# Sums in one PSUM bank in a seven-product down projection, and exponentials added by fours in every block of a transformer layer

## Chip, cores and metric

One Trainium2 chip; the kernel runs on one of its cores. The metric is device time in microseconds (us), the median of several runs. Engines: PE (TensorE, matmuls), DVE (VectorE), ACT (ScalarE), POOL (GpSimd), SP (SyncE, which issues most DMAs). A matmul writes PSUM, eight banks of 128 partitions x 512 float32; here four banks hold attention scores, one holds the attention accumulator, three ("lin") are shared by everything else.

## The reference

A pre-norm transformer layer in float32: x is (2, 1024, 1024), 32 heads of 32, FFN width 2752.

```python
def attn(x):
    qkv = (x @ qkvw + qkvb).reshape(B, S, 3, 32, 32)
    q, k, v = (qkv[:, :, i].transpose(0, 2, 1, 3) for i in range(3))
    probs = softmax(einsum('bhqd,bhkd->bhqk', q, k) / sqrt(32))
    ctx = einsum('bhqk,bhkd->bhqd', probs, v)
    return ctx.transpose(0, 2, 1, 3).reshape(B, S, H) @ ow + ob

def ffn(x):
    return (silu(x @ W_gate.T) * (x @ W_up.T)) @ W_down.T

x = x + attn(layernorm(x))
x = x + ffn(layernorm(x))
```

## The kernel before

The tokens are worked off in four blocks (batch b, half blk), 512 query tokens each. Attention of a block is 16 units of two heads; a unit has eight key tiles kt of 128 keys. For a key tile PE makes the scores (L510), ACT copies them to SBUF tile p (L529), DVE keeps the running maximum (L526). When all eight are there, DVE transposes and reduces the maximum (L549, L550), PE transposes it once more into a lin bank (L564), DVE reduces it to its negative (L565), and it goes through DRAM into a row m. Eleven key tiles behind the scores, `less_maximum` adds m (L580, on POOL, in the first block one of four on DVE), ACT takes the exponential (L589), and `values` multiplies with the values (L618).

The sum of the exponentials, the denominator of the softmax, comes from matmuls with a tile of ones into the other half of the same accumulator. To need fewer of these, neighbouring p tiles are first added in place (`add`, L603). In all blocks odd tiles take in the even one before them; in the first block (phase 0) every fourth tile also takes in the sum two tiles before it. The values are changed to match by `differences` (POOL, L594 and L597): if p1 holds p0+p1, then p0(v0-v1) + (p0+p1)v1 is what is wanted. So in phase 0 a run of four tiles needs four value calls and one call with ones, in phases 1 to 3 four and two (`summed`). Each call is four matmuls that run side by side in the array, of 256 columns. The adds are on DVE in phase 0; in phases 1 to 3 the add of kt 3 and 7 is on DVE, that of kt 1 and 5 on POOL.

The FFN of a block takes 21 chunks of 128 hidden rows and half a chunk, in parts of four chunks. A chunk is done by seven products of half size (Strassen in Winograd's form; L922, evicted mainly by DVE, L936 to L949), in place of eight. The down projection of the five whole parts is also done by seven products, each for two token tiles t (128 tokens), with two matmuls j of 512 columns each: `down7`, L1071. Its left factors are quarters of the hidden tile h and sums of them, which DVE makes in place in `sums_h` (L1040 to L1046). Each product goes into a lin bank of its own; DVE then adds it into the residual tile x in one or two places (`goes`: V1 to V4 are the four quarters of the output, product 1, 7 and 5 go to two of them; L1084, subtraction L1086). The part that is left over and the output projection are plain (L998, L780).

The order of the instructions of every engine is written out by the program: an `Emitter` interleaves a list of fill steps (projections, FFN) with the attention steps in equal beats. It runs a clock of estimated PE costs (`MM4` = 855 ns for one matmul of 512 columns), and `em.later(delay, ...)` emits a step once that clock has passed. The order of emission is the order of each engine's queue, which it works off in order. What has to wait for what, and which of a tag's buffers is free, is found by the tile framework from the uses of each tile. Attention of block 0 runs beside the projections, that of blocks 1 to 3 beside output projection and FFN of blocks 0 to 2; the FFN of block 3 is alone. Values of four tiles are emitted once the fourth is given as ("added", unit, kt), three beats after its `less_maximum`.

Weights of the down projection come by SP's queue into ten buffers of tag "D"; the list of loads follows `order`, and each matmul with t = 1 asks for the next load (`dst.next`).

Of the kernel before, what the change touches and what calls it, by code (L numbers as in the profile page):

```python
# [12 lines left out]
ALU = mybir.AluOpType  # L13
# [5 lines left out]
NH = 512  # L19
EPS = 1e-5  # L20
PART = 4
# [109 lines left out]
def preln_block_kernel(  # L131
# [14 lines left out]
    nc = tc.nc  # L146
# [13 lines left out]
    MM4, MM1 = 855.0, 230.0  # L160
# [36 lines left out]
    def lps(name, shape=(P, NH)):  # L197
        return psum.tile(list(shape), F32, tag="lin", bufs=3, name=name)
# [27 lines left out]
    WHOLE = (NFULL + 1) // PART  # L226
# [238 lines left out]
    class Unit:  # L465
# [111 lines left out]
        def less_maximum(self, kt):  # L577
            p = self.p[kt]
            eng = nc.vector if self.phase == 0 and kt % 4 == 3 else nc.gpsimd
            eng.tensor_tensor(p, p, self.m, ALU.add)  # L580
            em.later(3500.0, lambda: self.exponential(kt))
            if kt % 2 == 1:
                twice = self.phase == 0 and kt % 4 == 3
                em.later(8100.0, lambda: self.add(kt, 1), None if twice else ("added", self.n, kt))
                if twice:
                    em.later(9900.0, lambda: self.add(kt, 2), ("added", self.n, kt))
# [4 lines left out]
        def differences(self):  # L591

            v = self.v.rearrange("p (i a) n -> p i a n", a=2)
            nc.gpsimd.tensor_tensor(v[:, :, 0, :], v[:, :, 0, :], v[:, :, 1, :], ALU.subtract)  # L594
            if self.phase == 0:
                v = self.v.rearrange("p (i a) n -> p i a n", a=4)
                nc.gpsimd.tensor_tensor(v[:, :, 1, :], v[:, :, 1, :], v[:, :, 3, :], ALU.subtract)  # L597

        def add(self, kt, back):


            eng = nc.vector if self.phase == 0 or kt % RUN == RUN - 1 else nc.gpsimd
            eng.tensor_tensor(self.p[kt], self.p[kt], self.p[kt - back], ALU.add)  # L603

        def summed(self, kt):
            return kt % (4 if self.phase == 0 else 2) == (3 if self.phase == 0 else 1)

        def values(self, kt):


            if kt == 0:
                self.acc = psum.tile([P, NH], F32, tag="acc", bufs=1, name=f"acc_{self.name}")

            def columns(w, c, start, stop):
                for j in range(HPG):
                    part, h = divmod(j, 2)
                    q0 = h * NH + part * NQ
                    nc.tensor.matmul(  # L618
                        self.acc[j * HD : (j + 1) * HD, c : c + NQ],
                        w(h),  # L620
                        self.p[kt][:, q0 : q0 + NQ],
                        start=start,
                        stop=stop,
                        skip_group_check=True,
                    )

            v = lambda h: self.v[:, kt, h * HD : (h + 1) * HD]
            columns(v, 0, kt == 0, kt == NT - 1)
            if self.summed(kt):
                columns(lambda h: ones, NQ, False, kt == NT - 1)  # L630
            if kt == NT - 1:
                self.finish()
# [15 lines left out]
    def attention_steps(cuts):  # L648


        units = [Unit(n) for n in range(B * NS * UNITS)]
        lists = [Steps()]
        total = len(units) * NT
        q = lists[0]

        def load_step(k, i):
            if k < len(units):
                q.add(lambda: units[k].load(i), needs=("qk", units[k].b, units[k].g))

        for i in range(2):  # L660
            load_step(0, i)
        for n in range(total + NT + LAG + 3):
            if n in cuts:
                q = Steps()
                lists.append(q)
            k, kt = divmod(n, NT)
            if n < total:
                if kt == 1 or kt == 3:
                    load_step(k + 1, kt // 2)
                if n == 0:  # L670
                    q.add(lambda: em.later(9000.0, lambda: None, ("first",)))
                    q.add(lambda: None, needs=("first",))
                if kt == NT - 2:
                    q.add(units[k].load_v, needs=("v", units[k].b, units[k].hf))
            if n < total and kt % 2 == 0:
                q.add(lambda k=k, i=kt // 2: units[k].scores(i), MM4, beat=True)
            else:
                q.add(lambda: None, beat=True)
            k, kt = divmod(n - NT - LAG, NT)
            if 0 <= k < len(units):  # L680
                if kt == 0:
                    q.add(units[k].differences)
                q.add(lambda k=k, kt=kt: units[k].less_maximum(kt), needs=("max", k))
            k, kt = divmod(n - NT - LAG - 3, NT)
            if 0 <= k < len(units) and kt % RUN == RUN - 1:
                q.add(lambda: None, needs=("added", k, kt))
                for v in range(kt - RUN + 1, kt + 1):
                    cost = MM4 / 2 * (1 + units[k].summed(v))
                    q.add(lambda k=k, v=v: units[k].values(v), cost)
        return lists  # L690

# [155 lines left out]
    def ffn_steps(q, b, blk, st, turn):  # L847
# [36 lines left out]

        plain = {1: (0, 0), 2: (1, 0), 3: (1, 1)}
        dsums = {5: 0, 6: 1, 7: 2, 4: 3}
        order = (1, 2, 4, 7, 5, 6, 3)
        for pi in range(len(parts)):
            if pi < WHOLE:
                for n in order:  # L890
# [133 lines left out]
        def release(t, i):  # L1024
            x0, x1, x2, x3 = halves(t)
            if i == 0:
                nc.vector.tensor_tensor(x2, x3, x2, ALU.subtract)
            else:
                nc.vector.tensor_tensor(x1, x1, x3, ALU.add)
# [5 lines left out]
        def sums_h(pi, i):  # L1035
            a11, a12 = quarter_of(pi, 0, 0), quarter_of(pi, 0, 1)
            a21, a22 = quarter_of(pi, 1, 0), quarter_of(pi, 1, 1)
            if i == 0:
                st["s3"] = Sm(f"s3_{b}_{blk}_{pi}").rearrange("p (c n) -> p c n", c=2)
                nc.vector.tensor_tensor(st["s3"], a11, a21, ALU.subtract)  # L1040
            elif i == 1:
                nc.vector.tensor_tensor(a21, a21, a22, ALU.add)
            elif i == 2:
                nc.vector.tensor_tensor(a11, a21, a11, ALU.subtract)
            else:
                nc.vector.tensor_tensor(a12, a12, a11, ALU.subtract)  # L1046
# [7 lines left out]
            6: lambda pi: quarter_of(pi, 0, 0),  # L1054
            3: lambda pi: quarter_of(pi, 0, 1),
        }
        V1, V2, V3, V4 = (0, 0), (0, 1), (2, 0), (2, 1)
        goes = {
            1: ((V1, ALU.add), (V4, ALU.add)),
            2: ((V1, ALU.add),),  # L1060
            4: ((V3, ALU.add),),
            7: ((V2, ALU.subtract), (V4, ALU.add)),
            5: ((V3, ALU.add), (V4, ALU.add)),
            6: ((V4, ALU.add),),
            3: ((V2, ALU.add),),
        }

        def down7(pi, n, t, j):
            if j == 0:
                st["pd"] = lps(f"pd{n}_{b}_{blk}_{pi}_{t}")  # L1070
            nc.tensor.matmul(  # L1071
                st["pd"],
                lefts[n](pi)[:, j, t * P : (t + 1) * P],
                st["wp", pi, n, j],
                start=(j == 0),
                stop=(j == PART // 2 - 1),
            )
            if t == 1:
                dst.next()
            if j == PART // 2 - 1:  # L1080
                for (u, hf), op in goes[n]:
                    xs = st["x", t + u][:, hf * NH : (hf + 1) * NH]
                    if op == ALU.add:
                        nc.vector.tensor_tensor(xs, st["pd"], xs, op)  # L1084
                    else:
                        nc.vector.tensor_tensor(xs, xs, st["pd"], op)  # L1086

        def down_steps(pi):
            if pi < WHOLE:
                for n in order:  # L1090
                    for t in range(2):
                        for j in range(PART // 2):
                            q.add(lambda n=n, t=t, j=j: down7(pi, n, t, j), MM4)
                        if n == 3 and pi == WHOLE - 1:
                            q.add(lambda t=t: release(t, 0))
                    if n in (1, 2, 4, 7):
                        q.add(lambda i=(1, 2, 4, 7).index(n): sums_h(pi, i))
                return


            for hf in range(NHF):
                for t in range(TB):
                    for ci in range(len(parts[pi])):
                        q.add(lambda hf=hf, t=t, ci=ci: down(pi, hf, t, ci), MM4)
                    if hf == 0 and t < 2:
                        q.add(lambda t=t: release(t, 1))
# [246 lines left out]
```

## Time and profile before

| | us |
|---|---|
| median of 3 runs (lowest to highest) | 3282.67 (3280.46 to 3286.37) |
| the profiled execution | 3281.96 |
| its span, first to last instruction | 3280.2 |
| PE busy | 3217.5 (98%) |
| DVE busy | 1920.4 (59%) |
| POOL busy | 1758.6 (54%) |
| ACT busy | 1431.2 (44%) |
| mean granted TensorE clock | 0.994 |

The profile is of one execution. A group of instructions is told by its line in the kernel, its engine and its tiles (out<-in). "Busy" is the time in which at least one instruction of the group or engine ran. Matmul ends are modelled, with a tail that overlaps the next matmul, so distances between starts tell the rate better than durations. A float32 matmul shows as two records. A wait is the idle time of an engine just before an instruction, with the line that ended it.

### The profile page before, as it was taken

The numbers are of one execution on the slowest core, as the hardware profiler recorded it, in microseconds if no ns is written. First come the engines' busy times: TensorE is split into PE (matmuls) and PEld (weight loads), VectorE is DVE, ScalarE is ACT, GpSimd is POOL, SyncE is SP. The second block draws the span as 40 slices with busy tenths as digits, with TensorE's granted clock in tenths as the row PEclk, the third lists the DMA queues.
The fourth block names the chain that finished last, engine by engine and source line by source line (L and its number), as shares of the span: only waits on it lengthen the run. The fifth ranks groups of instructions, "written<-read, shape, count | busy, mean of one in ns | idle before, by whom it ended". The sixth has DMA issues, their size and how long they took to land. (4 is left out here: it accounts for less than half of the span.)

```text
span 3280.2 us, 43732 instructions
## 1 busy us (share of the span) xinstructions
PE 3217.5 (98%) x16320; PEld 1801.1 (55%) x16320; DVE 1920.4 (59%) x2478; ACT 1431.2 (44%) x1570; POOL 1758.6 (54%) x871
## 2 busy tenths in 40 slices
PE   8999999999999999999999999989999999999999
PEld 4444444444347655663466556634655566477775
DVE  2265676666356766666666666676666664344334
ACT  2244554444455545563655455545555554010000
POOL 0267776876676655568665555667765665200000
PEclk9999999999999999999999999999999999999999
DMA  4556766655534445446344444463444444544442
GB/s 155 171 184 193 226 192 203 200 180 161 158 99 135 142 151 146 146 146 200 107 142 145 139 141 137 145 192 110 137 145 146 146 138 140 184 151 153 153 152 97
DMA packets 337826, 507.29 MB, mean 155 GB/s; under 512 B 105424, under 2 KB 122064, under 8 KB 337616
## 3 DMA queue, kind: packets, MB, share of 16 engines
q1 hardware_dynamic: 281424, 405.91, 40.3%
q10 hardware_dynamic: 56192, 98.60, 9.8%
q8 instruction: 130, 2.13, 0.3%
q14 instruction: 80, 0.66, 0.1%
HBM read 429.14 MB, written 75.24 MB: 154 GB/s over the span
## 5 line engine op out<-in xcount | busy, mean ns | idle before, releaser
L580 POOL TENSOR_TENSOR p<-p,m 128x1024 f32<-128x1024 f32 x480 | 1180.8, 2483 | 13.6 <-DMA m<-d 13.4
L529 ACT COPY p<-s 128x1024 f32<-128x1024 f32 x512 | 516.7, 1011 | 872.1 <-DVE top L526 664.5
L526 DVE TENSOR_TENSOR top<-s,top 128x1024 f32<-128x1024 f32 x384 | 468.1, 1219 | 289.0 <-PE s L510 280.0
L589 ACT ACTIVATE p<-p 128x1024 f32<-128x1024 f32 x512 | 532.2, 1057 | 234.7 <-POOL p L580 206.8
L922 PE MATMUL p<-sum,m 128*128 128x256 f32 x2688 | 617.8, 383 | 4.9 <-DVE sum L904 3.3
L603 POOL TENSOR_TENSOR p<-p,p 128x1024 f32<-128x1024 f32 x96 | 227.2, 2367 | 658.9 <-ACT p L589 598.3
L922 PEld LDWEIGHTS p<-sum,m 128*128 128x128 f32 x2688 | 503.2, 190 | 124.7 <-issue 43.0
L922 PE MATMUL p<-xn2T,m 128*128 128x256 f32 x2016 | 473.5, 384 | 1.9 <-ACT gate L934 1.3
L370 PE MATMUL pq<-xnT,wqk 128*128 128x512 f32 x1024 | 463.7, 601 | 0.0
L1071 PE MATMUL pd<-wp,h 128*128 128x512 f32 x960 | 442.3, 607 | 8.3 <-DVE x L1084 6.4
L922 PEld LDWEIGHTS p<-xn2T,m 128*128 128x128 f32 x2016 | 378.2, 191 | 98.5 <-issue 45.4
L603 DVE TENSOR_TENSOR p<-p,p 128x1024 f32<-128x1024 f32 x192 | 306.2, 1595 | 134.1 <-ACT p L589 134.0
L370 PEld LDWEIGHTS pq<-xnT,wqk 128*128 128x128 f32 x1024 | 187.2, 190 | 252.8 <-issue 249.0
L1071 PEld LDWEIGHTS pd<-wp,h 128*128 128x128 f32 x960 | 179.3, 193 | 242.5 <-issue 203.4
L510 PE MATMUL s<-q,k 32*128 32x512 f32 x2048 | 300.8, 645 | 7.1 <-ACT p L529 7.0
L1084 DVE TENSOR_TENSOR x<-pd,x 128x512 f32<-128x512 f32 x360 | 236.9, 681 | 86.8 <-PE pd L1071 86.7
L618 PE MATMUL acc<-p,vals 128*32 128x256 f32 x4096 | 266.0, 383 | 1.8 <-DVE p L603 1.8
L1184 POOL TENSOR_TENSOR ws<-raw 128x512 f32<-128x512 f32 x62 | 93.7, 1512 | 299.9 <-DMA raw<-in_w_gu 170.5
L432 PE MATMUL pvv<-wv,xnT 128*128 128x512 f32 x512 | 233.3, 600 | 1.5 <-ACT xnT L266 1.5
L780 PE MATMUL po<-wo,ctx 128*128 128x512 f32 x512 | 234.6, 607 | 0.0
L618 PEld LDWEIGHTS acc<-p,vals 128*32 128x32 f32 x4096 | 120.1, 110 | 143.6 <-issue 70.2
L950 ACT ACTIVATE gate<-gate 128x512 f32<-128x512 f32 x84 | 52.9, 630 | 278.4 <-DVE gate L949 278.0
(96 smaller groups left out, 2451.3 us busy)
## 6 DMA issues: line engine op xcount, KB each, us to landing
m<-dws SPq DMA_DIRECT2D x336, 256.0 KB
m<-in_w_gu SPq DMA_DIRECT2D x252, 256.0 KB
wp<-ddn SPq DMA_DIRECT2D x160, 256.0 KB
m<-d SPq DMA_DIRECT2D x64, 512.0 KB
wp<-in_w_dn SPq DMA_DIRECT2D x120, 256.0 KB
raw<-in_w_gu ACTq DMA_DIRECT2D x84, 256.0 KB
dws<-ws ACTq DMA_DIRECT2D x84, 256.0 KB
x<-in_x SPq DMA_DIRECT2D x32, 512.0 KB
```

Of the source, the lines that this page charges most:

```text
L370: nc.tensor.matmul(ps, wqk[b, g, w, hk][:, k, :], xnT[b, s][:, kc, :], start=(kc == 0), stop=(kc == KC - 1),)
L510: nc.tensor.matmul(ps[a][:, h * NH : (h + 1) * NH], self.k[rows, i * P : (i + 1) * P], self.q[rows, :], start=True, stop=True,)
L526: nc.vector.tensor_tensor(self.top, s, self.p[0] if kt == 1 else self.top, ALU.max)
L529: nc.scalar.copy(self.p[kt], s)
L580: eng.tensor_tensor(p, p, self.m, ALU.add)
L589: nc.scalar.activation(self.p[kt], self.p[kt], AF.Exp, scale=SCALE)
L603: eng.tensor_tensor(self.p[kt], self.p[kt], self.p[kt - back], ALU.add)
L618: nc.tensor.matmul(self.acc[j * HD : (j + 1) * HD, c : c + NQ], w(h), self.p[kt][:, q0 : q0 + NQ], start=start, stop=stop, skip_group_chec ...
L780: nc.tensor.matmul(st["ps"], ctxT[b, blk][:, g, t * P : (t + 1) * P], st["w"][hf, g], start=(g == 0), stop=(g == G - 1),)
L922: nc.tensor.matmul(ps, mats[c, n][:, kc, :], rhs, start=(kc == 0), stop=(kc == hk - 1),)
L1071: nc.tensor.matmul(st["pd"], lefts[n](pi)[:, j, t * P : (t + 1) * P], st["wp", pi, n, j], start=(j == 0), stop=(j == PART // 2 - 1),)
L1084: nc.vector.tensor_tensor(xs, st["pd"], xs, op)
```

## The change

In attention, `add` by fours is done in all phases, so `differences` has its second subtraction and `values` has one call with ones for four tiles everywhere. Which engine does which add stays: the new second add (of kt 3 and 7, phases 1 to 3) is on DVE, emitted 9.9 us after `less_maximum`, and gives "added", which the first gave at 8.1 us.

In the down projection each output now gets one eviction for a bank, and three products add into the bank of another: 2 on top of 1, 6 on top of 7, 4 on top of 5. A bank is read after its first product (product 1 into V4, 7 from V2, 5 into V4), then the second product is accumulated on it (start=False), and it is read once more (1+2 into V1, 7+6 into V4, 5+4 into V3). The order of products is a list of turns (product, t), so that two other products stand between the two of a bank; (7, 0) and (2, 0) are one step, between which nothing else is emitted. The four sums of `sums_h` are emitted before the first product and behind (1, 0), (1, 1) and (2, 1), instead of behind products 1, 2, 4 and 7. The weights are loaded in the new order.

```diff
             if kt % 2 == 1:
-                twice = self.phase == 0 and kt % 4 == 3
+                twice = kt % 4 == 3
                 em.later(8100.0, lambda: self.add(kt, 1), None if twice else ("added", self.n, kt))
                 if twice:
                     em.later(9900.0, lambda: self.add(kt, 2), ("added", self.n, kt))
...
-            if self.phase == 0:
-                v = self.v.rearrange("p (i a) n -> p i a n", a=4)
-                nc.gpsimd.tensor_tensor(v[:, :, 1, :], v[:, :, 1, :], v[:, :, 3, :], ALU.subtract)
+            v = self.v.rearrange("p (i a) n -> p i a n", a=4)
+            nc.gpsimd.tensor_tensor(v[:, :, 1, :], v[:, :, 1, :], v[:, :, 3, :], ALU.subtract)
...
-            if self.summed(kt):
+            if kt % 4 == 3:
                 columns(lambda h: ones, NQ, False, kt == NT - 1)
...
-        order = (1, 2, 4, 7, 5, 6, 3)
+        order = (1, 2, 7, 6, 5, 4, 3)
...
         goes = {
-            1: ((V1, ALU.add), (V4, ALU.add)),
-            2: ((V1, ALU.add),),
-            4: ((V3, ALU.add),),
-            7: ((V2, ALU.subtract), (V4, ALU.add)),
-            5: ((V3, ALU.add), (V4, ALU.add)),
-            6: ((V4, ALU.add),),
-            3: ((V2, ALU.add),),
+            1: (V4, ALU.add),
+            2: (V1, ALU.add),
+            7: (V2, ALU.subtract),
+            6: (V4, ALU.add),
+            5: (V4, ALU.add),
+            4: (V3, ALU.add),
+            3: (V2, ALU.add),
         }
+        on_top = {2: 1, 6: 7, 4: 5}
+
+        turns = (
+            [(1, 0)], [(1, 1)], [(7, 0), (2, 0)], [(2, 1)], [(7, 1)], [(6, 0)], [(5, 0)], [(6, 1)],
+            [(5, 1)], [(4, 0)], [(3, 0)], [(4, 1)], [(3, 1)],
+        )
 
         def down7(pi, n, t, j):
-            if j == 0:
-                st["pd"] = lps(f"pd{n}_{b}_{blk}_{pi}_{t}")
+            key = "pd", on_top.get(n, n), t
+            if j == 0 and n not in on_top:
+                st[key] = lps(f"pd{n}_{b}_{blk}_{pi}_{t}")
             nc.tensor.matmul(
-                st["pd"],
+                st[key],
                 lefts[n](pi)[:, j, t * P : (t + 1) * P],
                 st["wp", pi, n, j],
-                start=(j == 0),
+                start=(j == 0 and n not in on_top),
                 stop=(j == PART // 2 - 1),
+                skip_group_check=True,
             )
...
-                for n in order:
-                    for t in range(2):
+                q.add(lambda: sums_h(pi, 0))
+                sums_behind = {(1, 0): 1, (1, 1): 2, (2, 1): 3}
+
+                def go(pair):
+                    for n, t in pair:
+                        for j in range(PART // 2):
+                            down7(pi, n, t, j)
+
+                for pair in turns:
+                    if len(pair) > 1:
+                        q.add(lambda pair=pair: go(pair), PART * MM4)
+                    else:
+                        n, t = pair[0]
                         for j in range(PART // 2):
                             q.add(lambda n=n, t=t, j=j: down7(pi, n, t, j), MM4)
-                        if n == 3 and pi == WHOLE - 1:
-                            q.add(lambda t=t: release(t, 0))
-                    if n in (1, 2, 4, 7):
-                        q.add(lambda i=(1, 2, 4, 7).index(n): sums_h(pi, i))
+                    if pair[-1] in sums_behind:
+                        q.add(lambda i=sums_behind[pair[-1]]: sums_h(pi, i))
+                    if pair[-1][0] == 3 and pi == WHOLE - 1:
+                        q.add(lambda t=pair[-1][1]: release(t, 0))
                 return
```

More of the change, by code (lines that the diff above doesn't have):

```diff
@@ L603, in add @@
             eng.tensor_tensor(self.p[kt], self.p[kt], self.p[kt - back], ALU.add)
-        def summed(self, kt):
-            return kt % (4 if self.phase == 0 else 2) == (3 if self.phase == 0 else 1)
         def values(self, kt):
@@ L687, in attention_steps @@
                 for v in range(kt - RUN + 1, kt + 1):
-                    cost = MM4 / 2 * (1 + units[k].summed(v))
+                    cost = MM4 / 2 * (1 + (v % 4 == 3))
                     q.add(lambda k=k, v=v: units[k].values(v), cost)
@@ L1080, in down7 @@
             if j == PART // 2 - 1:
[L1081 to L1086, printed above, removed]
+                (u, hf), op = goes[n]
+                xs = st["x", t + u][:, hf * NH : (hf + 1) * NH]
+                if op == ALU.add:
+                    nc.vector.tensor_tensor(xs, st[key], xs, op)
+                else:
+                    nc.vector.tensor_tensor(xs, xs, st[key], op)
         def down_steps(pi):
             if pi < WHOLE:
-                for n in order:
-                    for t in range(2):
+                q.add(lambda: sums_h(pi, 0))
[7 more added lines that the diff above has]
+                        q.add(lambda pair=pair: go(pair), PART * MM4)
+                    else:
+                        n, t = pair[0]
                         for j in range(PART // 2):
                             q.add(lambda n=n, t=t, j=j: down7(pi, n, t, j), MM4)
-                        if n == 3 and pi == WHOLE - 1:
-                            q.add(lambda t=t: release(t, 0))
-                    if n in (1, 2, 4, 7):
-                        q.add(lambda i=(1, 2, 4, 7).index(n): sums_h(pi, i))
+                    if pair[-1] in sums_behind:
+                        q.add(lambda i=sums_behind[pair[-1]]: sums_h(pi, i))
+                    if pair[-1][0] == 3 and pi == WHOLE - 1:
+                        q.add(lambda t=pair[-1][1]: release(t, 0))
                 return
```

## The prediction

> **What bounds the kernel now.** I read four views in this order: busy time by stage, the groups of instructions by shape, TensorE's own waits, and the order of time around single blocks. By stage (columns: length, then busy us and instruction count of PE, weight loads, DVE, ACT, POOL, then granted clock, DMA share, GB/s):
>
> ```profile
> 160.00:790.00 630.00, 625.75 (x2894) 259.86 (x2893) 407.28 (x378) 302.82 (x331) 456.94 (x242) 1.00 0.63 196
> 790.00:2800.00 2010.00, 1965.57 (x11290) 1149.08 (x11289) 1273.55 (x1664) 1059.45 (x1134) 1262.38 (x593) 0.99 0.48 143
> 2795.00:3280.00 485.00, 481.35 (x1736) 325.70 (x1728) 198.05 (x364) 29.27 (x56) 22.95 (x19) 1.00 0.46 147
> ```
>
> The first row is attention of the first block beside the projections, the second is attention of the other three blocks (48 units) beside output projection and FFN of the first three, the third is the last FFN alone. PE is busy 97.8% of the long stage and 99% of the others; DVE is at 63%, POOL at 63% there. So PE's work sets the time: a matmul taken away is a gain, DVE or POOL work matters only where PE comes to wait for it. How much PE waits in the long stage, and for whom:
>
> ```profile
> PE top L564 <- DVE part L550: 15.5, 9, 3.0
> PE pd L1071 <- DVE x L1084: 7.1, 12, 1.4
> PE s L510 <- ACT p L529: 7.0, 5, 2.6
> ...
> PE acc L618 <- DVE p L603: 1.5, 1, 1.5
> ```
>
> All of it is 44 us, and it is DVE being late for single moments, not DVE being full. A second price hangs on it: after some of these stalls the clock is halved. This stretch behind a stall shows it:
>
> ```profile
> 1821.33:1824.70 3.37, 2.86 (x4) 1.31 (x5) 3.24 (x6) 0.00 (x0) 0.00 (x0) 0.50 0.02 7
> ```
>
> The stall was 2.03 us and 3.4 us at half clock followed, so some 1.7 us of matmul time was lost behind it. Between 790 and 2800 us there are nine such stretches, six of 3.4 and three of 6.8 us, some 20 us in all; three of the short ones (1821, 1948, 2033 us; 5 us lost) lie in down projections. The Trainium skill's "TensorE: Matmul & The Clock Gate", section "Why this matters for your kernels", asks for no gap above about 3 us, since one idle window drops the clock; here stalls of 1.62, 2.03 and 2.70 us were followed by half clock, so by the page the downs would lose no clock at all, by the rows 5 us, and the rows decide.
>
> **The ones matmuls.** A run of four value tiles with its sums looks so, first in the last blocks (pairs, two calls with ones), then in the first (fours, one call):
>
> ```profile
> 2431.57 1.07 PE L618 MATMUL acc<-p,vals 128*32 128x256 f32 x16
> 2432.46 0.61 PE L618 MATMUL acc<-p,ones 128*32 128x256 f32 x8
> 2432.89 1.05 PE L618 MATMUL acc<-p,vals 128*32 128x256 f32 x16
> 2433.76 0.61 PE L618 MATMUL acc<-p,ones 128*32 128x256 f32 x8
> 2434.30 1.13 PE L922 MATMUL p<-xn2T,m 128*128 128x256 f32 x4
> ```
>
> ```profile
> 415.83 1.94 PE L618 MATMUL acc<-p,vals 128*32 128x256 f32 x32
> 417.58 0.61 PE L618 MATMUL acc<-p,ones 128*32 128x256 f32 x8
> 418.13 2.84 PE L370 MATMUL pq<-xnT,wqk 128*128 128x512 f32 x6
> ```
>
> From start to the next group: 2434.30-2431.57 = 2.73 us against 418.13-415.83 = 2.30 us, and 2.728 and 2.296 are the medians of the 96 and 32 such runs. The first becomes the second, 48 units x 2 runs = 96 times: 96 x 0.432 = **41.5 us less PE**. The other end is the busy time of the group below: 768 of 1792 records of 137.7 us are 59 us, but that counts the overlapped tail of every call, so I take 41.5.
>
> **What the fours cost.** Durations from the groups by shape:
>
> ```profile
> L603 DVE TENSOR_TENSOR p<-p,p 128x1024 f32<-128x1024 f32 x192 | 306.2, 1595 | 134.1 <-ACT p L589 134.0
> ...
> L1084 DVE TENSOR_TENSOR x<-pd,x 128x512 f32<-128x512 f32 x360 | 236.9, 681 | 86.8 <-PE pd L1071 86.7
> ...
> L618 PE MATMUL acc<-p,ones 128*32 128x256 f32 x1792 | 137.7, 379 | 0.0
> ...
> L597 POOL TENSOR_TENSOR vals<-vals 128x128 f32<-128x128 f32 x16 | 12.5, 782 | 1.3
> ```
>
> 96 more DVE adds at 1.60 us are 153 us of DVE. Beside POOL they vary (median 1.22, longest 3.44). The Trainium skill's "SBUF — State Buffer", section "Who interferes with whom", speaks against the edit: a DVE instruction with two SBUF inputs and a GpSimd one that reads SBUF block each other wholly. As an estimate by that page, with POOL 63% busy in instructions of 2.4 us, an add would wait 0.63 x 1.2 = 0.75 us on 1.22, 1.97 us each, 189 us in all; the row's mean is 1.60, so 153, and the row decides.
>
> Where does the second add (9.9 us after the subtraction, where the first stands at 8.1) touch PE? First at the value matmuls that read it: in the trace their distance from the end of the add has a median of 5.1 us over 96 runs, and four are under 2 us (0.05, 1.18, 1.78, 1.95). Moved back by some 1.9 us these would wait 1.9+0.7+0.1 = 2.7 us: **+3 us**. Then behind it on DVE's queue stand the evictions of the FFN products (0.42 us each). A product lasts 1.73 us and its PSUM buffer is wanted two products later; the time between eviction and reuse was under 1.3 us in 7 of 108 cases in each of the three blocks, at least 0.1, else mostly above 2.2 us. About 21 of 32 second adds of a block fall among products; each holds up one or two evictions: 21 x 1.5 x 7/108 = 2 hits of half a us, three blocks: **+3 us**. If all 96 adds hit, it would be 96 x 0.5 = 48 us, the end I keep for a rival. The negated maximum (L565) also stands behind the add; its row m has POOL waiting 5.0 us in the long stage and is wanted some five beats later, so nothing. POOL's 48 more differences are 48 x 0.78 = 38 us, covered by the 598 us that POOL waits for ACT's exponentials; without that cover up to 38 us of POOL, not of PE.
>
> **The down projection.** 28 matmuls a part before and after, so no PE work changes. DVE loses three evictions for each t: 20 parts x 2 x 3 = 120 x 0.68 = 82 us, 61 us of them in the long stage. There DVE goes from 1273 to 1273+153-61 = 1365 of some 1972 us, 69%: fuller, not the bound. The new waits: the second product of a bank starts after DVE has read the first. A quiet row of the last block, where DVE has nothing else, shows how long that takes:
>
> ```profile
> 3021.48 0.69 DVE L1084 TENSOR_TENSOR x<-pd,x 128x512 f32<-128x512 f32 x1 [0.94 <-PE pd L1071]
> ```
>
> The product that it evicts ends at 3021.28, so the bank is free 0.89 us later. With two products between there are 3.43 us, as with three buffers before. The one shorter place: with banks A and B held for products 1, and C by (7,0), (7,1) needs A after the eviction of (2,0), with only (2,1), 1.72 us, between; slack 0.83 us. In the last block that is enough. In the 15 parts beside attention a maximum (1.22 us) may stand ahead: 0.4 us on average, **+6**; four of them have the transpose of the maximum after three or four products, where it now waits for A, about 1 us each: **+4**. Against it, the double evictions of products 7 and 5 go, behind which evictions ended 3 to 5 us after their product; the stalls of later products in these rows (0.1 to 1.6 us, some 7 us, with one half-clock stretch 1.7) go, and some 1 us each where the transpose waited 2.03 and 2.70: **-10**. So the downs come to 0; ends -20 (all 15 us of stalls and 5 of clock gone, nothing new) and +56 (below). The pair glued together lets attention's steps wait up to 3.4 us; scores come every 10 us and their PSUM is freed about 6 us after, so a hit is rare: **+1**. The first h sum moves ahead of product 1: 0.7 us DVE, under 3.4 us of slack. The reordered weight loads keep their number and 10 buffers; PE waited 1.4 us once for one, so nothing.
>
> **Sum.** 3281.96 (span 3280.2 and 1.8 around it; the median of the runs is 3282.67) - 41.5 + 3 + 3 + 0 + 1 = **3247 us**, -1.1%; its own range 3230 to 3268.
>
> **Rivals.** (1) *The bank wait takes over*, 13%: in each of the 15 parts beside attention, between (2,0) and (7,1) or at the transpose, DVE is some 2 us late and half clock follows: 15 x (2.0+1.7) = 56 us, 3303 us. It decides from (41.5-7)/15 = 2.3 us for a part. For it: 2.03 and 2.70 us stalls in such parts, and three banks with two held. Against: S steps that brought maxima before these evictions now come behind the glued pair, and the sums before them are not more than now. (2) *DVE's fuller queue*, 9%: the 96 adds each cost PE 0.35 us among products: +34, 3281 us, no change. For: 69% busy in order. Against: margins above 2.2 us in most cases. (3) *The relief counts*, 12%: all stalls in the downs go: 3247-20 = 3227 us. For: backlogs of 4 to 5 us behind products 7 and 5. Against: the early ones come from maxima. That the saved evictions alone bring nothing is part of the forecast, for they were hidden.
>
> **How the numbers follow.** Forecast 66%, rivals 13, 9 and 12. The time is the forecast's, 3247. The range goes from 3226 (rival 3's middle; about 6% below) to 3284 (rival 1 and a little of rival 2 above, 14%). Beyond 0.2%, about what a measurement of this kernel can tell from none (3276 to 3289): faster 66+12+2 = 80%, within 7%, slower 13%.
>
> **What would show it.** Ones records 1024 instead of 1792 and every run of values at 2.30 us; L603 on DVE 288 times; evictions of pd 280 instead of 400, and PE's busy time down by about 41. Right if PE's waits stay near 45 us in the long stage; rival 1 shows as pd waiting on x after (2,0) with more half-clock stretches, rival 2 as p L922 waiting for gate or up evictions. A loss of PE time outside waits and clock would make all this wrong.

## The result, and the profile after

The changed kernel takes 3315.38 us (median of 4, 3314.23 to 3321.16), the kernel before 3281.57 us beside it (median of 4): a ratio of 1.0105, 95% interval 1.009 to 1.012. It is about 34 us slower; the forecast was 35 us faster, and the stated range ended at 3284.

| us | before | after |
|---|---|---|
| profiled execution | 3281.96 | 3314.23 |
| its span | 3280.2 | 3312.4 |
| PE busy | 3217.5 | 3199.3 |
| DVE busy | 1920.4 | 2002.3 |
| POOL busy | 1758.6 | 1799.7 |
| mean granted TensorE clock | 0.994 | 0.987 |
| PE waits beside attention of blocks 1 to 3 | 44 | 95 |
| lost in half-clock stretches there (half of their length) | 20 in 9 | 44 in 18 |

The last three rows hold the result. The stages after, in the same columns as before (length; busy us and count of PE, weight loads, DVE, ACT, POOL; clock, DMA share, GB/s):

```profile
160.00:790.00 630.00, 626.31 (x2895) 259.44 (x2894) 409.99 (x380) 304.08 (x333) 456.36 (x243) 1.00 0.62 197
790.00:2830.00 2040.00, 1944.73 (x10519) 1126.12 (x10518) 1370.68 (x1672) 1058.56 (x1132) 1304.00 (x640) 0.98 0.46 141
2845.00:3310.00 465.00, 463.62 (x1689) 317.62 (x1687) 169.97 (x316) 27.41 (x54) 17.99 (x15) 1.00 0.45 146
```

The first and last stage are as they were. The long one is where the time went, and DVE is not full in it: 1371 of 2040 us, 67%. Three groups, by shape:

```profile
L602 DVE TENSOR_TENSOR p<-p,p 128x1024 f32<-128x1024 f32 x288 | 473.0, 1642 | 136.4 <-ACT p L589 136.0
...
L1090 DVE TENSOR_TENSOR x<-pd,x 128x512 f32<-128x512 f32 x240 | 164.2, 685 | 127.7 <-PE pd L1076 127.3
...
L614 PE MATMUL acc<-p,ones 128*32 128x256 f32 x1024 | 80.1, 385 | 0.0
```

Ones records fell from 1792 to 1024, the adds rose by 96, the evictions at this line fell by 120: the change does what it says. PE's busy time fell by 18 us and not by the 41 given as a sign: matmuls at half clock take longer, and 24 us more were lost so. All 128 runs of values now last 2.30 us in the median. PE's waits in the long stage, after (us in total, times, longest):

```profile
PE acc L614 <- DVE p L602: 33.0, 18, 8.9
PE pd L1076 <- DVE s L1036: 29.0, 10, 4.2
PE top L564 <- DVE part L550: 9.7, 4, 3.5
...
PE pd L1076 <- DVE x L1090: 1.0, 2, 0.8
```

Two waits are new: the fourth value tile waits for the second add (before: 1.5 us), and product 7 waits for the first h sum s3 (before: nothing). Waits for evictions, which rival 1 was about, are 1.0 us, less than the 7.1 before. The books of the two profiled executions close: 41.5 us of ones matmuls went, 95-44 = 51 us of waits and 44-20 = 24 us of clock came, together +33; the span grew by 32.2.

**Product 7.** The order of time at the start of one down projection, first PE, then DVE, then POOL:

```profile
1722.15 3.60 PE L1076 MATMUL pd<-wp,h 128*128 128x512 f32 x8
1728.71 3.78 PE L1076 MATMUL pd<-wp,s 128*128 128x512 f32 x4 [2.97 <-DVE s L1036]
...
1722.35 0.42 DVE L945 TENSOR_TENSOR gate<-p,gate 128x256 f32<-128x256 f32 x1 [0.77 <-PE p L918]
1724.32 1.58 DVE L948 TENSOR_TENSOR h<-gate,up 128x512 f32<-128x512 f32 x1 [1.55 <-ACT gate L946]
1725.83 2.83 DVE L1036 TENSOR_TENSOR s<-h 128x512 f32<-128x512 f32 x1
...
1720.70 10.17 POOL L580 TENSOR_TENSOR p<-p,m 128x1024 f32<-128x1024 f32 x4
```

PE has two products (1, 0) and (1, 1), 3.43 us, and then wants s3. But s3 stands on DVE behind the end of the chunk just finished: DVE waits for ACT's silu, multiplies (L948), and only then comes to s3, whose inputs were ready a chunk before. On top both instructions are stretched, to 1.58 and 2.83 us, beside four POOL instructions in a row. In the last block, where POOL has little to do, the same order is quiet, and s3 is there 0.8 us before PE wants it:

```profile
2975.63 0.69 DVE L948 TENSOR_TENSOR h<-gate,up 128x512 f32<-128x512 f32 x1 [0.70 <-ACT gate L946]
2976.24 0.68 DVE L1036 TENSOR_TENSOR s<-h 128x512 f32<-128x512 f32 x1
...
2977.74 1.88 PE L1076 MATMUL pd<-wp,s 128*128 128x512 f32 x4
```

The 15 first sums of the long stage had a mean of 2.03 us, against 0.73 at their old place, and fall into two kinds. Ten overlapped POOL and took 1.51 to 2.85 us: these are the ten for which PE waited. The other five did not overlap POOL and took 0.68 to 0.69 us, and PE did not wait for them. Behind the stall shown first the clock was halved:

```profile
1728.10:1734.70 6.60, 5.99 (x7) 2.53 (x8) 5.12 (x6) 0.00 (x0) 2.76 (x2) 0.50 0.00 0
```

The four records of product 7 took 3.78 us there, against 1.88 in the row of the last block.

**The second add.** DVE, then PE, at one run of values (the two L602 are first and second add):

```profile
1597.23 2.50 DVE L602 TENSOR_TENSOR p<-p,p 128x1024 f32<-128x1024 f32 x1
1599.65 0.68 DVE L788 TENSOR_TENSOR x<-po,x 128x512 f32<-128x512 f32 x1
1600.25 1.21 DVE L526 TENSOR_TENSOR top<-s,top 128x1024 f32<-128x1024 f32 x1
1601.38 1.27 DVE L237 BATCH_NORM_STATS2 st_f<-x 128x6 f32<-128x512 f32 x2
...
1603.46 0.81 DVE L249 TENSOR_SCALAR xn<-x,mv_f,rstd_f 128x1024 f32<-128x1024 f32 x1
1604.19 1.22 DVE L602 TENSOR_TENSOR p<-p,p 128x1024 f32<-128x1024 f32 x1
...
1600.47 1.50 PE L614 MATMUL acc<-p,vals 128*32 128x256 f32 x24
1605.46 1.08 PE L614 MATMUL acc<-p,vals 128*32 128x256 f32 x8 [3.48 <-DVE p L602]
```

Three value tiles run and the fourth stands still for 3.5 us. The second add itself takes 1.22 us; what makes it late is all that was emitted between the two adds in 1.8 us of the program's clock and takes DVE 4.5 us. Over the 96 pairs the second add ended 2.96 us after the first in the mean (median 2.82, longest 7.33).

### The profile page after: what moved, and what is told of

Its sections match the earlier page's. It is cut to its first block, busy times and chain, and to the rows that moved or that the text cites. A ratio compares the mean times of both kernels' runs of the same rounds, so it can differ in the third digit from the quotient of the medians.

```text
span 3312.4 us, 42256 instructions
## 1 busy us (share of the span) xinstructions
PE 3199.3 (97%) x15552; PEld 1778.3 (54%) x15552; DVE 2002.3 (60%) x2454; ACT 1431.6 (43%) x1570; POOL 1799.7 (54%) x919
## 3 DMA queue, kind: packets, MB, share of 16 engines
q8 instruction: 124, 2.03, 0.3%
## 5 line engine op out<-in xcount | busy, mean ns | idle before, releaser
L580 POOL TENSOR_TENSOR p<-p,m 128x1024 f32<-128x1024 f32 x480 | 1194.5, 2511 | 14.4 <-DMA m<-d 7.5
L918 PE MATMUL p<-sum,m 128*128 128x256 f32 x2688 | 621.0, 384 | 5.1 <-DVE neg L565 2.6
L602 POOL TENSOR_TENSOR p<-p,p 128x1024 f32<-128x1024 f32 x96 | 227.8, 2373 | 649.4 <-ACT p L589 631.9
L918 PEld LDWEIGHTS p<-sum,m 128*128 128x128 f32 x2688 | 503.7, 190 | 129.0 <-issue 46.5
L602 DVE TENSOR_TENSOR p<-p,p 128x1024 f32<-128x1024 f32 x288 | 473.0, 1642 | 136.4 <-ACT p L589 136.0
L918 PE MATMUL p<-xn2T,m 128*128 128x256 f32 x2016 | 474.8, 384 | 2.8 <-DVE sum L827 1.9
L918 PEld LDWEIGHTS p<-xn2T,m 128*128 128x128 f32 x2016 | 378.0, 191 | 102.0 <-issue 44.3
L614 PE MATMUL acc<-p,vals 128*32 128x256 f32 x4096 | 254.9, 385 | 34.3 <-DVE p L602 34.0
L1090 DVE TENSOR_TENSOR x<-pd,x 128x512 f32<-128x512 f32 x240 | 164.2, 685 | 127.7 <-PE pd L1076 127.3
```

Of the source, the lines that this page charges most:

```text
L614: nc.tensor.matmul(self.acc[j * HD : (j + 1) * HD, c : c + NQ], w(h), self.p[kt][:, q0 : q0 + NQ], start=start, stop=stop, skip_group_chec ...
L918: nc.tensor.matmul(ps, mats[c, n][:, kc, :], rhs, start=(kc == 0), stop=(kc == hk - 1),)
```

## The experiments

All times below are medians; the ratio is against runs of the kernel before on the same chip, whose medians were 3281.6 to 3285.8. "The fours" are the half of the change in attention, "the down" is the half in the down projection, "s3" is the first h sum. Theory A, which I formed from the profile after, takes the two waits as separate costs; its rival B says that DVE is fuller and late as a whole. Theory C, that one wait hides another, was added after `e3_s3early`.

**The two halves of the change alone.** `e1_fours` is the kernel before with these lines:

```diff
-                twice = self.phase == 0 and kt % 4 == 3
+                twice = kt % 4 == 3
...
-            return kt % (4 if self.phase == 0 else 2) == (3 if self.phase == 0 else 1)
+            return kt % 4 == 3
```

and the second subtraction in all phases. `e2_down` is the change without them.

> Fours in all blocks, down projection as before. Theory A (two new waits: PE waits for the second add at the fourth value tile, 33 us and some 10 us of half clock behind it, and for the first h sum at product 7, 29 us and some 17 us of half clock): the 41.5 us of ones matmuls go, the value waits of some 43 us come, no wait at a product 7; time within 15 us of before, 3270 to 3297. Theory B (DVE is late as a whole because it is fuller): without the 61 us that the saved evictions give back in the long stage it is later still, over 3300.

> The down projection of the change, fours only in the first block. Theory A: the waits for the first h sum and their half clock cost 46 us, the 20 us that downs lose now go; 3282+46-20 = 3308, with PE waiting 25 to 30 us for the h sum. Theory B: DVE has 61 us less to do in the long stage, so no slower than before, 3270 to 3285.

Measured: 3298.42 us (ratio 1.0048, 1.003 to 1.0066) and 3297.36 us (1.0046, 1.0031 to 1.0061). Each half costs some 16 us, and neither brings the gain. The fours alone are just outside A's bounds, at B's edge; the down alone falls between the two. Their waits:

```profile
PE acc L617 <- DVE p L602: 39.2, 20, 8.0
PE top L564 <- DVE part L550: 13.3, 8, 3.5
PE pd L1070 <- DVE x L1083: 12.6, 17, 1.8
```

```profile
PE pd L1080 <- DVE s L1040: 26.5, 10, 4.4
PE top L564 <- DVE part L550: 8.2, 5, 3.0
```

The first is of the fours, the second of the down alone: each has its own one of the two new waits. In the down alone PE waits 60 us in the long stage, against 44 before, and loses 20 us to half clock, as before: its 16 us are waits, and the 17 us of half clock that A gave the h sum are not there. B's point that DVE has less to do in the down alone is true and did not help.

**The gain by itself.** Two kernels leave the second add out in the last three blocks, so that the sums there lack two of four exponentials (and so does one of the products with the values); all else of the fours stays.

```diff
-                    em.later(9900.0, lambda: self.add(kt, 2), ("added", self.n, kt))
+                    em.later(
+                        9900.0,
+                        (lambda: self.add(kt, 2)) if self.phase == 0 else (lambda: None),
+                        ("added", self.n, kt),
+                    )
```

> Fours in all blocks with the down projection of before, but the second add is left out in the last three blocks (two of four exponentials are missing from the sum there); the ones matmuls are as few as in the change. Prices the gain by itself: if the 41.5 us are right, 3282-41.5 = 3241, between 3234 and 3250. Over 3265, the gain was never there and the second add isn't what gave it back.

> The change with the same second adds left out. Prices the new down projection where DVE is not fuller: as the down alone cost 16 us on the kernel before, 3241+16 = 3257, between 3248 and 3267, with some 25 us of waits for the first h sum. At 3241 the down would cost nothing but for the adds, and the fuller DVE would be the one cause.

Measured: 3250.39 us with the old down (0.9898, 0.9881 to 0.9915) and 3268.03 us with the new one (0.9953, 0.9936 to 0.997). Both are within 1 us of the upper bound of what was expected, just above it. The gain is there: 33 us, with an interval of 28 to 39, less than 41.5; PE's waits in the long stage were 9 us over the kernel before, which is about the rest. The six numbers make a table:

| us | old down | new down | the new down costs |
|---|---|---|---|
| pairs, as before | 3282 | 3297 | 16 |
| fours without the second add | 3250 | 3268 | 18 |
| fours | 3298 | 3315 | 17 |
| the second add costs | 48 | 47 | |

The parts add up: -33 + 48 + 17 = +32. The gain of the fours and the cost of their add were of one size, and the down came on top.

**Curing one wait at a time.** `e3_s3early` emits the first h sum before the products of the chunk, not behind them:

```diff
             if c % PART == 0:
                 q.add(lambda pi=c // PART: alloc_h(pi))
+            if c % PART == 0 and 0 < c < NFULL - 1:
+                q.add(lambda pi=c // PART - 1: sums_h(pi, 0))
+            if c == NFULL and len(parts) - 2 < WHOLE:
+                q.add(lambda: sums_h(len(parts) - 2, 0))
...
-                q.add(lambda: sums_h(pi, 0))
```

`e4_vlater` takes the steps of `values` out of beat n-NT-LAG-3 and puts them, with the beat, ahead of the scores of the beat behind it.

> The change, with the first h sum emitted before the products of the chunk that the down projection follows, instead of right before the down. Theory A: PE's wait at product 7 goes, 29 us and 17 us of half clock: 3315-46 = 3269, between 3260 and 3280. Theory B: the lateness turns up at the next instruction; 3300 or more.

> The change, with the values of four tiles emitted one beat (some 5 us) later, right before the next scores. Theory A: the value waits go but for what is left of the two over 5 us: 33 to some 6 us, half clock 10 to some 5: 3315-32 = 3283, between 3273 and 3292. Theory B: 3300 or more.

Measured: 3308.12 us (1.0079, 1.0063 to 1.0094) and 3282.49 us (0.9999, 0.9989 to 1.0009). The second is what A said. The first refutes A: the wait went, and the time fell by 7 us, where A had 46; B had 3300 or more. Waits of the early sum:

```profile
PE acc L614 <- DVE p L602: 46.7, 23, 8.7
PE top L564 <- DVE part L550: 15.7, 7, 3.5
PE top L564 <- DVE x L1090: 7.9, 5, 2.4
```

No wait at product 7, but the value waits rose from 33.0 to 46.7 and those at the transpose of the maximum from 13.4 to 23.6: of 29 us, 24 came back at two other lines. A reading of this, not shown by itself, is that DVE caught up while PE stood at product 7, and that PE without that stop reaches the next late instruction sooner. Hence theory C and the next runs: both cures (`e5_both`), the later values with the old down (`e6_fours_vlater`), the later values on the kernel before (`e7_vlater_alone`), and both cures with `turn` and its DMAs at 12500, 14000 and 16500 (`e8_turn`).

> Both: first h sum early and values one beat later. Theory A (each wait is its own cost): the 23 us for the h sum and some 8 us of half clock go from 3282.5: 3250. Theory C (DVE's queue is behind for stretches; a wait of PE lets it catch up, and without that wait PE meets the next late instruction, as when the h sum alone was moved): the wait for the h sum goes to zero, the transposes of the maximum and the evictions take most of it, 3270 to 3282.

> Fours in all blocks and values one beat later, with the down projection of before. Theory A: the 39 us of value waits and some 9 us of half clock go from 3298: 3250. Theory C: half of it turns up elsewhere: 3270 to 3280. Against the change with later values (3282.5): lower by 20 to 30 under A, since the 23 us for the h sum are not there.

> The kernel before with values one beat later, nothing else: a control. Value waits are 1.5 us there, so under A and C nothing: 3277 to 3287. If it is faster by over 10 us, the later values are a gain of their own and not the cure of the fours' wait.

> Both as before, and PE's transpose of the maximum with the two DMAs behind it 2 us later. Theory A: PE's waits of some 14 us there go too, with half clock 5: 3235. Theory C: some 5 to 10 us less than without it.

Measured: 3272.00 (0.9963, 0.9951 to 0.9975), 3271.81 (0.9971, 0.9958 to 0.9985), 3282.06 (0.9995, 0.9983 to 1.0006), 3280.05 us (0.9995, 0.9984 to 1.0006). C holds for the first two, the control is neutral, and the later transpose made it worse, so no theory was right there. What PE waits for with both cures:

```profile
PE top L564 <- DVE part L550: 9.8, 7, 2.0
PE pd L996 <- DVE x L1007: 8.6, 4, 3.8
PE top L564 <- DVE x L1092: 8.6, 5, 2.4
PE pt_f L258 <- ACT gate L932: 7.5, 3, 4.6
PE p L920 <- DVE gate L934: 6.2, 7, 2.2
```

It is spread over five lines and more. Two of them, L996 (the part of the down projection that is left over) and L258 (transposes of the layer norm), stood at 0.4 us together in the change. They come with the later values: on the kernel before these alone brought 6.0 and 5.0 us there. Why is not shown.

**The second add on POOL.** One line of `add`, on both kernels with later values:

```diff
-            eng = nc.vector if self.phase == 0 or kt % RUN == RUN - 1 else nc.gpsimd
+            eng = nc.vector if self.phase == 0 or (kt % RUN == RUN - 1 and back == 1) else nc.gpsimd
```

> The change with first h sum early, values one beat later and the second add of the last three blocks on POOL instead of DVE: DVE has some 133 us less to do in the long stage, POOL 227 us more. Theory C (what was left, 3272, is DVE's lateness): 3252 to 3264. If POOL's queue becomes the late one (subtraction, exponential and value waits on POOL): 3275 or more.

> Fours, values one beat later, the second add on POOL, the down projection of before. Theory C: 3250 to 3262, close to the run before it in this call, since both downs came out alike with the adds on DVE (3272). If POOL is late: 3275 or more.

Measured: 3273.12 (0.9969, 0.9957 to 0.9981) and 3286.27 us (1.0008, 0.9996 to 1.0021). Both miss theory C; the second lies where a late POOL was expected, the first between the two. Value waits for POOL are 25 and 29 us in their profiles, and DVE's relief brought no gain.

**A smaller shift.** The value steps stay in their beat and wait half a beat there, so that the scores keep their place:

```diff
+                q.add(lambda k=k, kt=kt: em.later(2600.0, lambda: None, ("late", k, kt)))
+                q.add(lambda: None, needs=("late", k, kt))
                 q.add(lambda: None, needs=("added", k, kt))
```

It was run with the early sum on the change (`g2_halfbeat`), on the fours with the old down (`g3_halfbeat_olddown`), alone on the kernel before (`g4_halfbeat_alone`), and on the change as it is (`g5_after_halfbeat`). `g1_down_s3early` is the new down alone with the early sum.

> The new down projection alone (fours only in the first block) with the first h sum early. Theory A (the down's 16 us are PE's waits for that sum): 26 us of waits and some of the half clock go, 3297-30 = 3267, between 3260 and 3277. Theory C (DVE behind, the wait moves): 3285 to 3297, with the wait at other lines.

> The change with the first h sum early and the values half a beat (2.6 us) later, the scores where they were. With a whole beat 3272 was left, some of it from scores right behind values. Under C some 25 us of value waits stay (the ones over 2.6 us) but others shrink: 3265 to 3285. Under A 3250.

> The same half beat on fours with the down projection of before: 3265 to 3280 under C; the two downs within 10 us of each other.

> The kernel before with values half a beat later, nothing else: a control. Value waits are 1.5 us there, so if the shift only cures the second add's wait: 3277 to 3290. If it is faster by over 10 us, the shift is a gain of its own.

> The change with values half a beat later and the first h sum where the change has it. Theory A: against the same with the sum early (3252) PE's wait at product 7 is back, as between the two downs without fours (3297 against 3279): 3252+18 = 3270, between 3262 and 3280. If the sum's place counts only through the values' wait: 3252 to 3258.

| | us | ratio, 95% interval |
|---|---|---|
| `g1_down_s3early` | 3278.73 | 0.9982, 0.9972 to 0.9992 |
| `g2_halfbeat` | 3252.21 | 0.9909, 0.9888 to 0.993 |
| `g3_halfbeat_olddown` | 3259.88 | 0.9925, 0.9902 to 0.9949 |
| `g4_halfbeat_alone` | 3271.99 | 0.9962, 0.9948 to 0.9976 |
| `g5_after_halfbeat` | 3262.60 | 0.9933, 0.9918 to 0.9948 |

`g2_halfbeat` came out at A's 3250 and not in C's range, `g3_halfbeat_olddown` 5 us below C's, and `g5_after_halfbeat` just inside A's. C thus fits where the values wait or a whole beat moves them, and A does better once half a beat has taken the value waits away (0.4 us in the first and the last, 1.8 in the other).

The early sum takes 19 us off the new down where DVE is not fuller (3297 to 3279), missing A's bounds by 2 us, and 10 us off with later values (3263 to 3252), where a wait of 32 us for s3 went:

```profile
PE pd L1078 <- DVE s L1038: 32.0, 12, 4.3
```

```profile
PE top L564 <- DVE part L550: 11.7, 5, 3.7
PE top L564 <- DVE x L1092: 11.3, 5, 2.9
PE pd L1078 <- DVE x L1092: 10.4, 10, 1.7
PE p L920 <- DVE gate L934: 8.7, 9, 1.7
```

The first row is of the change with values half a beat later, the others of the same with the early sum (its slowest execution, 3261 us): s3 is gone, and smaller waits stand at four lines. With both cures the change takes 3252 us, faster than both kernels, by 0.9% and 1.9%. But the control says that 13 us of this are a gain of the half beat on the kernel before, where there was hardly a value wait to cure. Against that control the cured change is 20 us better.

Where the half beat helps the kernel before is not in the waits: those of the long stage are 52 us against 44. It is in PE's busy time, 3197.3 us against 3217.5. In 124 of 128 runs the values now stand directly ahead of scores, before in none:

```profile
1502.70 0.61 PE L618 MATMUL acc<-p,ones 128*32 128x256 f32 x8
1503.25 1.14 PE L510 MATMUL s<-q,k 32*128 32x512 f32 x8
1504.32 4.56 PE L1073 MATMUL pd<-wp,h 128*128 128x512 f32 x10
```

So PE changes 644 times, not 768, between the large products (128*128) and the small matmuls of attention. A change has a price in the trace before: from the start of one record of `pd` to the next it is 429 ns, to a score behind it 522; for the chunk products `p` it is 216 and 309. 124 x 93 ns is 11.5 us, an estimate from these medians, near the 13. It is not the whole account, for the whole beat alone (`e7_vlater_alone`) has the same 644 changes and gained nothing; why is open.

Nor do the fours with the half beat reach what they gain without their second add. 3250 less the 13 us would be 3237 (an estimate that takes the two as independent), and `g3_halfbeat_olddown` has 3260. The value waits are 1.8 us there, but waits of pd for evictions are 20.6 us, against 11.9 without the second add: a part of that add's price is then probably B's fuller queue, and it stays.

## Why the prediction was wrong

**The ones matmuls** were right in kind and in count: 96 runs went from 2.73 to 2.30 us. With the second adds left out the kernel gained 33 us of the 41.5.

**"Moved back by some 1.9 us ... +3 us" is the step that failed most.** The second add was priced by its own length and the 1.8 us between the two emissions. DVE works in order, and what stands between the two adds moves with it: the shift was 2.96 us in the mean and 7.33 at worst, the first adds had themselves lost ground (their distance to the fourth value tile fell from a median of 5.1 to 3.9 us), and 24 of 96 runs ended without any margin. 33.0 us of waits came in place of 3, and half clock behind the longest. Leaving the add out gave 47 to 48 us. The count of four small margins was right; that the margin is used up by the queue between, not by the instruction, was missed.

**"The first h sum moves ahead of product 1: 0.7 us DVE, under 3.4 us of slack" failed too.** Only the sum's cost in DVE time was looked at. The slack of 3.43 us had to hold everything ahead of it in the queue: the last eviction of the chunk, ACT's silu, the multiplication and then s3, and beside POOL the last two took 1.58 and 2.83 us in the stretch shown. The 0.7 us is the quiet duration; that DVE adds vary beside POOL was seen, and charged to the adds alone. With quiet durations the chain of the stretch shown would have ended about when PE came, and the one of the last block ended 0.8 us before. 29.0 us of waits came, none were priced.

**"So the downs come to 0"** was 16 to 18 us too low, all of it this sum: with the sum early the new down alone is 0.2% faster than the kernel before. The terms that went into that zero were nearly right in the change where they were about banks: waits of pd for evictions fell from 7.1 to 1.0 us, and the transpose's waits for the bank are 3.7 us against the 4 that I priced. But the stop at s3 hides a part of this: with the sum early, the new down alone has 3.7 and 9.9 us there.

**Rival 1** gave the sign and some of the size (3303 against 3315), with half clock in its price, but by luck, for it had the wrong place: PE stood two products into the part, at s3, and not for a bank, and more of the loss came at the values. **Rival 2**, the fuller queue, was priced as hits among the FFN products; DVE's lateness struck at the values instead. **Rival 3** did not come.

**The half clock** was seen, and charged to a rival alone. It made 24 of the 75 us that the books set against the 41.5, and the forecast had no half clock behind a new wait.

**The +3 for the FFN products** was small, and so was what came: PE's waits for all causes went from 6.8 us (L922 before) to 7.9 us (L918 after), those for gate and up evictions from 1.8 to 0.9.

## What to carry to other kernels

On an engine that works in order, price a new instruction by where its queue stands when a consumer wants it: add up everything ahead of it, with its waits for third engines, and not its own time against a mean distance. When an edit brings a result nearer to its consumer, emit the producer as soon as its inputs are there; and move consumers with a lengthened chain, here by half a beat, with a control run of that move alone, for it may bring a gain of its own. Waits of a full in-order engine stand in for one another, so curing one of two shows less than its size: 29 us of waits removed gave 7 us, and 10 to 19 us once the other was small or gone.

## What the runs showed of the hardware

The price of a stall is more than its length, and grows with it. Over the 19 profiled kernels of this case, from 160 us on, a half-clock stretch of 3.4 us or more ran during the stall or began within 3.4 us behind it at 12 of 105 PE stalls of 1.0 to 1.3 us, 39 of 182 of 1.3 to 2 us, 54 of 85 of 2.0 to 2.7 us, 60 of 71 of 2.7 to 3.5 us and 46 of 47 longer ones. The count does not tell apart what a second stall nearby added. There is no sharp bound, and more than half of the stalls of 2.0 to 2.7 us cost at least 1.7 us on top, half of such a stretch. The Trainium skill's "TensorE: Matmul & The Clock Gate", section "Why this matters for your kernels", allows gaps up to some 3 us; by these rows 105 of 372 stalls between 1.0 and 2.7 us already had half clock at or behind them, and the rows decide.

A DVE instruction of 128x512 with both inputs in SBUF that takes 0.68 us alone took 2.83 us beside an unbroken run of four POOL instructions (`less_maximum`) in 10.17 us. The eviction next to it in the same run, which reads PSUM, took its usual 0.68 us:

```profile
1728.58 0.68 DVE L1090 TENSOR_TENSOR x<-pd,x 128x512 f32<-128x512 f32 x1
```

It is so throughout the change. The 76 second adds that did not overlap POOL took 1.15 to 1.22 us, the 20 that did had a median of 2.21 and a longest of 3.37; of the first adds 39 took 1.21 to 1.23, and 57 beside POOL had a median of 2.30. None of the 240 evictions at L1090 took more than 0.69 us, beside POOL or not. Which instruction becomes slow thus moves with its place in the order. That two such instructions hold each other up is what the Trainium skill's "SBUF — State Buffer", section "Who interferes with whom", states; the traces agree, and show that the price is far from even.
